# Graph attention over sorted edges: features turned three blocks ahead, and the PSUM banks divided anew

## The chip, the cores and the metric

The kernel runs on one core of a Trainium2 chip. The metric is the device time of one execution in microseconds (us), lower is better. Five engines work side by side, each through its own list of instructions in order: PE (TensorE, matrix products and transposes), DVE (VectorE), ACT (ScalarE), POOL (GpSimd) and SP (SyncE, which here only issues DMAs). They wait for each other through semaphores. SBUF is the large on-chip memory; PSUM is the small one that PE writes into, and it has eight banks, each of which holds 512 float32 values per partition.

## The reference, cut to what matters

There are 12,500 nodes with 128 features and 212,500 edges, sorted by their destination. A node has 8 heads of 16 dimensions.

```python
h = relu(layernorm(x))
q, v = h @ Wq.T + bq, h @ Wv.T + bv            # one row per node
k = edge_attr @ Wk.T + bk                      # one row per edge
qs, qd = q[src], q[dst]
in_m, out_m, diag_m = sum(qs * k), sum(qd * k), sum(qs * qd)      # per head: 24 logits per edge
score = (segment_softmax(in_m / 4, dst) + segment_softmax(out_m / 4, dst)
         + segment_softmax(diag_m / 4, dst)) * distance ** lam
y = segment_sum(score * v[dst], dst)
out = x + leaky_relu(y @ Wo.T + bo, 0.1)
```

The softmax over the edges of one destination needs the largest logit of each destination. Since edges are sorted, these are runs of neighbouring edges.

## The kernel before, in words

The program holds two paths. `ordered_path` always runs; it also looks at the data and writes a flag, and `general_path` runs only if the edges are not as the first path needs them, which they are here.

**Before the loop.** All nodes are loaded and normalized, q is computed for all of them and stored in DRAM in `q_table`. A second table, `q3_table`, holds q as the sum of three bfloat16 terms.

**The tiling of the edges.** 512 edges are one block (`BE`), four edges on each of 128 partitions (`JN` = 4). The 415 blocks of the loop are cut into five strands (`S` = 5) of 83 blocks (`G`). The loop counts steps g; `t = g // 5` is the round and `s = g % 5` the strand. Five blocks, one of each strand, make a round, and what is done once per round handles 5 x 24 = 120 rows: a row of PSUM or SBUF for each strand and logit, along 512 edges.

**What a step does** (lines 1487 to 1547). For the block g + 15 POOL gathers q[src] from `q_table`, 128 rows with each of four indirect DMAs (L691), into one of 22 buffers `qq`. The four are allowed to start after certain PE instructions of earlier steps (`behind`). For the block g + 1 PE computes k into one half of a `kq_ps` tile (`project`, L1155 for the bias and L1157), and q[dst] into the other half (`spread_q`, L1165), the product of a matrix of zeros and ones (`oh`) with the rows of `q3_table` in `win`; ACT copies q[dst] to SBUF as `qd` (L1168). For the block g + 2 PE turns the edge features by four transposes into the PSUM tile `eT_ps` (`turn`, L1148), and ACT copies them to SBUF as `eT` (L1150), from which `project` of the next step takes its weights. For the block g DVE multiplies (`logits`, L1178 and L1179) and, at s = 1, 3 and 4, sums over the 16 dimensions of a head (L1184). ACT makes `oh` for block g + 3 (`one_hots`, L1142 and L1143).

**What a round does.** The logits of a round go through a chain that is spread over the steps of the next two rounds:

- s = 0: PE turns the logits to rows (`turn_logits`, L1205, tile `l_ps`); DVE scans along the edges for the running maximum of each destination (`scan_on`, `u`, L1238), with a row `far` that holds a large negative number where a new destination begins, and a short scan of 64 edges (`head`, L1243). ACT copies `far` to a PSUM tile `far_ps` (`spread_far`, L1249).
- s = 1: DVE scans back, from the last edge to the first (`scan_back`, `m`, L1256), with the row from `far_ps`, where there is one, or else from `far` in SBUF.
- s = 2: PE turns `m` back (`turn_max`, L1326, tile `m_ps`); DVE subtracts (L1334), and ACT takes the exponential (L1335).
- s = 3: PE makes two `d_ps` tiles (`show_ends`, L1360), which ACT turns into zeros and ones (`sel`, L1363 and L1364); DVE multiplies by the edge weights (`weigh_powers`, L1346).
- s = 4: PE sums over the edges of a destination (`to_rows`, L1374, tile `w_ps`), ACT copies the rows (L1379), and SP stores them (L1390).

Between these, nodes whose sums are complete are finished in groups of 512 (`Nodes`, two such groups of steps in most pairs of rounds once enough sums are there): a `node_ps` tile for a transpose at s = 1 (L1074, copied by ACT at L1077) and one for a product at s = 4 (`project_v` and `project_o`, L1080 and L1082). DVE's L1346, L1279, L1282 and L1107 take both operands from SBUF; most of the others take one from PSUM.

**PSUM.** Of the eight banks four belong to the two `kq_ps` tiles, one to `eT_ps`, and three are shared in turn by all small tiles (`small`, L1197): `l_ps`, `far_ps`, `node_ps`, `m_ps`, both `d_ps` and `w_ps`. A new small tile takes the bank of the third before it and waits until that one has been read.

**What sets the order.** `pin` (L596) ties every instruction to the one before it on its engine, so the order on each engine is that of the program text. SP issues the loads in this order too: the edge features of a round are one DMA of 1280 KB (`fetch_edges`, L679, two buffers), the places of the destinations one of 640 KB (`fetch_places`, L636).

**After the loop** (from L1549) the last rounds go through the same chain, and five groups of nodes that could not be finished earlier are (`rest`).

Of the kernel before, what the change touches and what calls it, by code (L numbers as in the profile page):

```python
# [7 lines left out]
F32 = mybir.dt.float32  # L8
# [464 lines left out]
def ordered_path(ctx: ExitStack, tc: tile.TileContext, flag, x, src, dst, edge_attr, edge_weight,  # L473
# [20 lines left out]
    N, F = x.shape  # L494
    E = src.shape[0]
    P = 128
    NI = -(-N // P)
    NP = P * NI
    BE, JN = 512, 4
# [23 lines left out]
    def parts_of(u):  # L523

        return [s for s in range(S)
                if (s == 0 or START * s - NEAR < UN * (u + 1))
                and (s == S - 1 or UN * u <= START * (s + 1) + NEAR)]
# [61 lines left out]
    end = S * G  # L589
# [6 lines left out]
    def pin(inst):  # L596

        engine = str(inst.ins.engine)
        if engine in pinned:
            tc.add_manual_dep(inst.ins, pinned[engine], mybir.DependencyInfo(  # L600
                mybir.DependencyClass.NoSync, mybir.DependencyReason.DATA), reason="in order")
        pinned[engine] = inst.ins.name
        return inst
# [72 lines left out]
    def fetch_edges(t):  # L676
        if t < G:
            ea = eas[t] = load.tile([P, S, JN * F], F32, name="ea")
            pin(nc.sync.dma_start(  # L679
                ea, edge_attr[:end * BE, :].rearrange("(s b p j) f -> p s b (j f)", s=S, b=G, p=P)  # L680
                [:, :, t, :]))

    def gather(g, of=range(JN)):
        if g < end:
            if 0 in of:
                qqs[g] = gath.tile([P, JN, F], F32, name="qq")
            qq = qqs[g]
            s, t = g % S, g // S
            for j in of:
                at = raw_i[:, t, s, j:j + 1] if g < RAW else src_i[:, s * G + t, j:j + 1]  # L690
                rows = pin(nc.gpsimd.indirect_dma_start(  # L691
                    out=qq[:, j, :], out_offset=None, in_=x if g < RAW else q_table,
                    in_offset=bass.IndirectOffsetOnAxis(ap=at, axis=0)))
                if g < RAW:
                    tc.add_manual_dep(rows.ins, pinned[sums_of], mybir.DependencyInfo(
                        mybir.DependencyClass.Sync, mybir.DependencyReason.SCHED_ONLY),
                        reason="one for each group of nodes")
                if (g - LOOK, j) in behind:
                    tc.add_manual_dep(rows.ins, behind[g - LOOK, j], mybir.DependencyInfo(
                        mybir.DependencyClass.Sync, mybir.DependencyReason.SCHED_ONLY),  # L700
                        reason="close behind the products")
# [330 lines left out]
    class Nodes:  # L1032
# [39 lines left out]
        def turn(self, to):  # L1072
            for b in range(self.n):
                pin(nc.tensor.transpose(to[:, b, :], self.h[:, b, :], ident))  # L1074
            if self.hT is None:
                self.hT = fin.tile([P, JN, P], F32, name="hT")
            pin(nc.scalar.copy(self.hT[:, :self.n], to[:, :self.n]))  # L1077
# [48 lines left out]
    with tc.tile_pool(name="work", bufs=2) as work, \  # L1126
            tc.tile_pool(name="scan", bufs=2) as scan, \
            tc.tile_pool(name="ps", bufs=1, space=PSUM) as ps:
        kqs, eTs, qds, ohs, lTs, prods = {}, {}, {}, {}, {}, {}

        def bank(g, i):

            if g not in kqs:
                kqs[g] = ps.tile([P, 2, JN, F], F32, name="kq_ps", bufs=2)
            return kqs[g][:, i]

        def one_hots(g):

            if g < end:
                oh = ohs[g] = work.tile([K3, BE], BF, name="oh", bufs=5)  # L1140
                d = places[g // S][:K3, g % S, :]
                pin(nc.scalar.activation(d, d, AF.Abs, bias=before[:K3]))  # L1142
                pin(nc.scalar.activation(oh, d, AF.Relu, bias=1.0, scale=-1.0))  # L1143

        def turn(g):
            eT_ps = ps.tile([P, JN, P], F32, name="eT_ps", bufs=1)
            for j in range(JN):
                pin(nc.tensor.transpose(eT_ps[:, j, :], eas[g // S][:, g % S, j * F:(j + 1) * F], ident))  # L1148
            eT = work.tile([P, JN, P], F32, name="eT", bufs=2)
            pin(nc.scalar.copy(eT, eT_ps))  # L1150
            eTs[g] = eT

        def project(g):
            k_ps = bank(g, 0)
            pin(nc.tensor.matmul(k_ps, ones3, bk3, start=True, stop=False))  # L1155
            for j in range(JN):
                pin(nc.tensor.matmul(k_ps[:, j, :], eTs[g][:, j, :], wk, start=False,  # L1157
                                     stop=(j == JN - 1)))
            del eTs[g]

        def spread_q(g):
            s, d = g % S, st[g // S]
            qd_ps = bank(g, 1)
            for j in range(JN):
                pin(nc.tensor.matmul(qd_ps[:, j, :], ohs[g][:, j * P:(j + 1) * P],  # L1165
                                     d["win"][:, s, :], start=(j == 0), stop=(j == JN - 1)))
            qds[g] = work.tile([P, JN, F], F32, name="qd")
            pin(nc.scalar.copy(qds[g], qd_ps))  # L1168
            del ohs[g]

# [23 lines left out]
            nc.vector.memset(ends_t[-1][0:1, :], 1.0)  # L1194

        def small(shape, name):
            return ps.tile(shape, F32, name=name, tag="small", bufs=3)  # L1197

        l_end = scan.tile([R, HEAD], F32, name="l_end", bufs=1)
        nc.vector.memset(l_end, 0.0)  # L1200
# [195 lines left out]
        def later(f, t, *more):  # L1396
            if 0 <= t < T:
                f(t, *more)

        def nodes_before(t, s):  # L1400

            new, old = pairs.get(t - t % 2), pairs.get(t - t % 2 - 2)
            if new and t % 2 == 1 and s == 4:
                new.project_v(small([P, JN, F], "node_ps"))
            if old and t % 2 == 0 and s == 4:
                old.project_o(small([P, JN, F], "node_ps"))
# [56 lines left out]

        def hold(of, apart=False):
            if apart:
                of.held = ps.tile([P, JN, F], F32, name="eT_ps", bufs=1)
            else:
                of.held = banks.pop(0)
            of.product(of.held, bv3, wv)
# [12 lines left out]
        project(0)  # L1482
        spread_q(0)
        turn(1)
        one_hots(1)
        one_hots(2)
        for g in range(end):
            s, t = g % S, g // S
            nodes_before(t, s)
            gather(g + LOOK)  # L1490
            if s == 0:
                fetch_edges(t + 1)
            if g + 1 < end:
                project(g + 1)
                behind[g + 1, 0] = pinned[products]
                spread_q(g + 1)
                behind[g + 1, 1] = pinned[products]
            if g + 2 < end:
                turn(g + 2)
                behind[g + 1, 2] = pinned[products]  # L1500
            logits(g)
            one_hots(g + 3)
            if s == 0:
                if t > 0:
                    turn_logits(t - 1)
                    scan_on(t - 1)
                later(select, t - 2)
                later(spread_far, t - 2)
            elif s == 1:
                later(scan_back, t - 2)  # L1510
                if t == 1:
                    logits_few()
            elif s == 2:
                later(turn_max, t - 2)
                later(powers, t - 2)
                fetch_places(t + 2)
            elif s == 3:
                later(show_ends, t - 2)
                later(weigh_powers, t - 2)
                other_terms(t, s)  # L1520
                fetch(t + 2)
            else:
                later(to_rows, t - 2)
            ahead, k = (t + 2, s - 3) if s > 2 else (t + 1, s + 2)
            if ahead > 1:
                fetch_rows(ahead, [k])
            later(put_rows, t - 2 if s == 4 else t - 3, [(s + 1) % S])
            if t == G - 1:
                if 0 < s < 4:
                    select(G - 3 + s)  # L1530
                elif s == 4:
                    for i in (G - 2, G - 1, G):
                        show_ends(i)
            behind[g + 1, 3] = pinned[products]
            nodes_between(t, s)
            if s < 3:
                other_terms(t, s)
            if g == 12 * S:
                examine()
            begin_rest(g - (end - BEGIN))  # L1540
            if g < S:
                of = [u for u in range(NU) if g in parts_of(u)]
                pin(nc.scalar.dma_start(
                    sums[g][of[0] * UN:(of[0] + len(of)) * UN].rearrange(
                        "(n p) i c -> p n (i c)", p=P),
                    blank[:, None, :].to_broadcast([P, 2 * len(of), 2 * 2 * H3])))
# [31 lines left out]
        for r in (2, 3):  # L1578
            hold(rest[r])
# [69 lines left out]
```

## Time and profile before

| | us |
|---|---|
| median of three runs | 2208.59 |
| lowest and highest | 2208.17 and 2213.11 |
| profiled execution | 2207.89 |
| its span, from the first instruction to the last | 2206.0 |
| mean granted TensorE clock | 0.781 of full speed |
| last gather of q[src] starts | 2136.02 |

How to read the profile: a row of the costliest groups has a line of the kernel, the engine, the operation, the tile written and the tiles read, the count, then the busy time of all, the mean of one in ns, and the idle time of the engine just before them with what ended most of it. A row of the waits has the engine, tile and line that waited, what it waited for, and the total, the number and the longest of these waits in us. A row of the timeline has the start, the duration in us, the engine, line, operation and tiles, and in brackets the idle time before it. A row for one line of the kernel has its count and the smallest, median and largest duration in ns, the first and the last start in us, and the shapes. A row of the stretches has the stretch, its length, the busy time and number of the instructions asked for, the granted clock, the DMA share and GB/s.

### The profile page before, as it was taken

How to read it: one execution, taken by the hardware profiler on the slowest of the kernel's cores; microseconds unless marked ns; L12 is line 12 of the kernel's file. 1: busy time of each engine (PE TensorE's matmuls, PEld its weight loads, DVE VectorE, ACT ScalarE, POOL GpSimd, SP SyncE). 2: the span in 40 equal slices, each digit the busy share in tenths (PEclk: the TensorE clock that was granted, in tenths of full speed). 3: DMA queues.
4: the chain of work that ended last, by engine and by line, in shares of the span. 5: the costliest groups of instructions: out<-in, count | busy, mean ns of one | idle time of the engine just before them, and what ended most of it. 6: DMA issues, size and time to landing. Idle time of an engine off the chain costs nothing.

```text
span 2206.0 us, 34366 instructions
## 1 busy us (share of the span) xinstructions
PE 1731.1 (78%) x10289; PEld 1377.7 (62%) x10289; DVE 1953.7 (89%) x2106; ACT 1406.7 (64%) x2617; POOL 1587.6 (72%) x1676
## 2 busy tenths in 40 slices
PE   7678777777887877878887787778887888778886
PEld 5456565665666666656666666666665666666664
DVE  8669999999999998899889999999989898889894
ACT  8656666666666666666666666666666666666671
POOL 3577777777777777777777777777777777777750
PEclk9757888788788788777777778787778777777776
DMA  9585555455455555554555555554556445555531
GB/s 267 165 255 167 159 154 175 143 168 168 145 161 178 159 153 170 163 169 148 155 159 175 164 155 153 178 163 145 162 165 178 149 148 149 172 148 151 154 101 58
DMA packets 306061, 355.65 MB, mean 161 GB/s; under 512 B 118195, under 2 KB 225661, under 8 KB 305557
## 3 DMA queue, kind: packets, MB, share of 16 engines
q1 hardware_dynamic: 237258, 238.26, 35.0%
q0 software_dynamic: 53184, 108.92, 17.4%
q10 hardware_dynamic: 15424, 6.19, 1.1%
q8 instruction: 83, 1.36, 0.3%
q14 instruction: 112, 0.92, 0.1%
HBM read 321.34 MB, written 31.85 MB: 160 GB/s over the span
## 4 chain that ended last, share of the span: by engine, by line
PE 36%; DVE 31%; DMA 13%; issue 11%; ACT 4%; POOL 3%; SPq 1%; DVEq 0%; ACTq 0%; POOLq 0%
PE kq_ps L1157 13%; DMA qq<-q_table,src_i 12%; DVE lT L1184 10%; DVE prod L1179 9%; PE w_ps L1374 6%; PE eT_ps L1148 5%; DVE prod L1178 5%; PE kq_ps L1155 3%; PE node_ps L1082 3%; DVE u L1238 3%; POOL qq L691 3%; PE kq_ps L1165 3%; PE d_ps L1360 2%; ACT xq L919 1%; PE l_ps L1205 1%
## 5 line engine op out<-in xcount | busy, mean ns | idle before, releaser
L691 POOL DMA_INDIRECT qq<-q_table,src_i x1636 | 1557.9, 952 | 505.8 <-issue 242.0
L1157 PEld LDWEIGHTS kq_ps<-wk,eT 128*128 128x128 f32 x3320 | 531.7, 244 | 377.6 <-issue 164.9
L1184 DVE TENSOR_REDUCE lT<-prod 128x192 f32<-128x3072 f32 (+1 forms) x249 | 702.1, 2820 | 8.5
L1157 PE MATMUL kq_ps<-wk,eT 128*128 128x128 f32 x3320 | 628.0, 347 | 11.5 <-ACT eT L1150 10.6
L1168 ACT COPY qd<-kq_ps 128x512 f32<-128x512 f32 x415 | 242.1, 583 | 432.0 <-PE kq_ps L1165 399.2
L1179 DVE TENSOR_TENSOR prod<-qq,kq_ps 128x1024 f32<-128x1024 f32 x415 | 504.1, 1215 | 13.0 <-issue 9.8
L1155 PE MATMUL kq_ps<-b,ones 3*128 3x512 bf16 x415 | 188.0, 453 | 217.3 <-DVE prod L1179 217.1
L1148 PE MATMUL eT_ps<-ident,ea 128*128 128x128 f32 x1660 | 327.3, 333 | 0.6 <-ACT att_t L806 0.6
L1142 ACT ACTIVATE relb<-relb,before 114x512 bf16<-114x512 bf16 x415 | 302.6, 729 | 0.0
L1178 DVE TENSOR_TENSOR prod<-qd,kq_ps 128x512 f32<-128x512 f32 x415 | 280.2, 675 | 12.2 <-ACT qd L1168 7.4
L1143 ACT ACTIVATE oh<-relb 114x512 bf16<-114x512 bf16 x415 | 261.3, 630 | 13.3
L1150 ACT COPY eT<-eT_ps 128x512 f32<-128x512 f32 x415 | 243.8, 588 | 39.4 <-PE eT_ps L1148 38.7
L1148 PEld LDWEIGHTS eT_ps<-ident,ea 128*128 128x128 f32 x1660 | 231.9, 176 | 0.9 <-ACT att_t L806 0.9
L1374 PE MATMUL w_ps<-back,sel 128*114 128x144 f32 (+1 forms) x1344 | 214.4, 321 | 16.0 <-DVE back L1346 10.6
L1374 PEld LDWEIGHTS w_ps<-back,sel 128*114 128x114 f32 (+1 forms) x1344 | 206.7, 212 | 23.3 <-ACT h L1064 5.8
L1326 PE MATMUL m_ps<-ident,m 120*128 120x120 f32 x332 | 70.8, 347 | 169.6 <-DVE m L1256 169.5
L1165 PE MATMUL kq_ps<-win,oh 114*128 114x128 bf16 x1660 | 201.9, 257 | 2.3 <-DMA win<-q_table 2.3
L1238 DVE TENSOR_TENSOR_SCAN u<-far,u,l_ps 120x512 f32<-120x512 bf16 x82 | 104.8, 1278 | 90.9 <-PE l_ps L1205 83.2
L1335 ACT ACTIVATE back<-back 128x480 f32<-128x480 f32 x83 | 50.1, 604 | 200.5 <-DVE back L1334 200.5
L1165 PEld LDWEIGHTS <-oh 114*128 114x128 bf16 x1660 | 162.9, 119 | 15.7 <-issue 2.6
L1326 PEld LDWEIGHTS m_ps<-ident,m 120*128 120x128 f32 x332 | 50.2, 215 | 192.4 <-DVE m L1256 191.2
L1256 DVE TENSOR_TENSOR_SCAN m<-far_ps,head,u 120x512 f32<-120x512 f32 x81 | 103.2, 1274 | 0.0
(192 smaller groups left out, 1435.4 us busy)
## 6 DMA issues: line engine op xcount, KB each, us to landing
ea<-in_edge_attr_dram SPq DMA_DIRECT2D x83, 1280.0 KB
relb<-rel_d SPq DMA_DIRECT2D x83, 640.0 KB
qq<-q_table,src_i POOLq DMA_INDIRECT x1636
win<-q_table SPq DMA_DIRECT2D x415, 28.5 KB
far<-far_d SPq DMA_DIRECT2D x84, 120.2 KB
q_table<-more_q SPq DMA_DIRECT2D x40, 192.0 KB
sums<-rows SPq DMA_DIRECT2D x412, 7.1 KB
q_table<-xq SPq DMA_DIRECT2D x24, 256.0 KB
```

Source lines behind the costliest of these rows:

```text
L691: rows = pin(nc.gpsimd.indirect_dma_start(out=qq[:, j, :], out_offset=None, in_=x if g < RAW else q_table, in_offset=bass.IndirectOffsetOn ...
L1142: pin(nc.scalar.activation(d, d, AF.Abs, bias=before[:K3]))
L1143: pin(nc.scalar.activation(oh, d, AF.Relu, bias=1.0, scale=-1.0))
L1148: pin(nc.tensor.transpose(eT_ps[:, j, :], eas[g // S][:, g % S, j * F:(j + 1) * F], ident))
L1150: pin(nc.scalar.copy(eT, eT_ps))
L1155: pin(nc.tensor.matmul(k_ps, ones3, bk3, start=True, stop=False))
L1157: pin(nc.tensor.matmul(k_ps[:, j, :], eTs[g][:, j, :], wk, start=False, stop=(j == JN - 1)))
L1165: pin(nc.tensor.matmul(qd_ps[:, j, :], ohs[g][:, j * P:(j + 1) * P], d["win"][:, s, :], start=(j == 0), stop=(j == JN - 1)))
L1178: pin(nc.vector.tensor_mul(prod[:, :, 2, :], qds[g], kqs[g][:, 0]))
L1179: pin(nc.vector.tensor_mul(prod[:, :, 0:2, :], qqs[g][:, :, None, :].to_broadcast([P, JN, 2, F]), kqs[g].rearrange("p i j f -> p j i f")))
L1184: pin(nc.vector.tensor_reduce(lTs[t][:, :, lo:s + 1, :].rearrange("p j s c -> p j (s c)"), prods[0][:, :, :s + 1 - lo].rearrange("p j s i ...
L1374: pin(nc.tensor.matmul(w_ps[:, i].rearrange("p s c -> p (s c)"), d["sel"][:n, j, lo:lo + 3, :].rearrange("p s w -> p (s w)"), d["back"][:n ...
```

## The change

It has four parts. `turn` runs for block g + 3 instead of g + 2, with two `eT_ps` banks and four `eT` buffers, and a set of transposes moves ahead of the loop; `qd` gets three buffers instead of two. The edge features are fetched at s = 2 for the round after the next instead of at s = 0 for the next one. The small tiles share two banks instead of three. And `spread_far` isn't called any more, so that `scan_back` always takes `far` from SBUF.

```diff
         def turn(g):
-            eT_ps = ps.tile([P, JN, P], F32, name="eT_ps", bufs=1)
+            eT_ps = ps.tile([P, JN, P], F32, name="eT_ps", bufs=2)
...
-            eT = work.tile([P, JN, P], F32, name="eT", bufs=2)
+            eT = work.tile([P, JN, P], F32, name="eT", bufs=4)
...
-            qds[g] = work.tile([P, JN, F], F32, name="qd")
+            qds[g] = work.tile([P, JN, F], F32, name="qd", bufs=3)
...
         def small(shape, name):
-            return ps.tile(shape, F32, name=name, tag="small", bufs=3)
+            return ps.tile(shape, F32, name=name, tag="small", bufs=2)
...
-                of.held = ps.tile([P, JN, F], F32, name="eT_ps", bufs=1)
+                of.held = ps.tile([P, JN, F], F32, name="eT_ps", bufs=2)
...
         turn(1)
+        turn(2)
...
-            if s == 0:
-                fetch_edges(t + 1)
+            if g == 0:
+                fetch_edges(1)
+            if s == 2:
+                fetch_edges(t + 2)
...
-            if g + 2 < end:
-                turn(g + 2)
+            if g + 3 < end:
+                turn(g + 3)
                 behind[g + 1, 2] = pinned[products]
...
                 later(select, t - 2)
-                later(spread_far, t - 2)
```

## The prediction

> **What bounds the kernel now.** I began with the page's busy times and its costliest groups.
>
> ```profile
> span 2206.0 us, 34366 instructions
> PE 1731.1 (78%) x10289; PEld 1377.7 (62%) x10289; DVE 1953.7 (89%) x2106; ACT 1406.7 (64%) x2617; POOL 1587.6 (72%) x1676
> L691 POOL DMA_INDIRECT qq<-q_table,src_i x1636 | 1557.9, 952 | 505.8 <-issue 242.0
> ```
>
> By these DVE is the bound and POOL has room. The waits of POOL say otherwise: once the gathers from q_table run, none before them is longer than 0.3 us, whatever releaser is named.
>
> ```profile
> POOL qq L691 <- issue: 242.0, 794, 0.3
> POOL qq L691 <- DMA qq<-q_table,src_i: 115.6, 379, 0.3
> POOL qq L691 <- PE kq_ps L1165: 28.6, 94, 0.3
> ```
>
> 0.30 us is thus a fixed gap. Next the gathers alone: their rate in one stretch, their number against the blocks multiplied by DVE (L1179) up to 400 us and from 1300 us on, and the end of the loop in the timeline.
>
> ```profile
> 400.00:1000.00 600.00, 454.42 (x478) 0.79 0.53 162
> ...
> L691 POOL DMA_INDIRECT qq<-q_table,src_i x252: 940/944/2768, 78.2 to 399.5; - x126
> L1179 DVE TENSOR_TENSOR prod<-qq,kq_ps x61: 1202/1214/1218, 111.1 to 396.7; 128x1024 f32<-128x1024 f32 x61
> ...
> L691 POOL DMA_INDIRECT qq<-q_table,src_i x669: 940/944/1367, 1299.3 to 2136.0; - x168
> L1179 DVE TENSOR_TENSOR prod<-qq,kq_ps x169: 1205/1215/1222, 1299.8 to 2134.4; 128x1024 f32<-128x1024 f32 x169
> ...
> 2136.02 0.94 POOL L691 DMA_INDIRECT qq<-q_table,src_i  x1 [0.30 <-issue]
> 2140.07 1.21 DVE L1179 TENSOR_TENSOR prod<-qq,kq_ps 128x1024 f32<-128x1024 f32 x1
> ```
>
> Undisturbed a gather comes every 0.944 + 0.303 = 1.247 us; measured it is 600 / 478 = 1.255, from 78.2 us to 2137. A block takes four, so 5.02 us, and a round of five blocks 25.1 us. At 400 us the gathers of (252 + 24) / 4 = 69 blocks were out (24 are the raw ones before the loop) and 61 blocks multiplied: POOL led by 8. After 1300 us both go at one pace (669 / 4 = 167 against 169), and DVE's last product starts 3 us after the last gather has been issued. **POOL is the bound**, a saturated chain from 78 to 2137 us. DVE is close behind it, and I read its waits to see how close.
>
> ```profile
> DVE u L1238 <- PE l_ps L1205: 83.2, 49, 4.0
> DVE prod L1179 <- issue: 9.8, 5, 2.4
> DVE prod L1179 <- DMA qq<-q_table,src_i: 3.2, 4, 1.2
> PE kq_ps L1157 <- ACT eT L1150: 10.6, 5, 4.1
> ```
>
> Only 9.8 + 3.2 = 13 us of DVE's idle time stand at the product that takes the gathered rows. Without them DVE's own chain would have ended at about 2140 - 13 = 2127 us. Two chains of nearly equal length: whatever lengthens either one shows. The profiled execution took 2207.89 us (span and 1.9 us around it), 0.7 under the median of 2208.59; I add to 2207.9.
>
> **The turning three blocks ahead.** The same 415 x 4 transposes and copies run in the same places of each step; one set moves ahead of the loop. What it can remove is PE's wait for a turned block: 10.6 us, 5 times (above). The much longer waits of the weight loads at the same line overlap the bias product and are not PE's. I take 0; at most -10.6, on DVE's chain only. The two eT buffers, the third qd and the ACT copy of far (0.58 us x 81) are no cost: ACT is busy 64%. Every POOL instruction stays where it was, and no gather waits for the PE steps that release it. The edge load moves two steps later in a round but a round further ahead, past the SP queue's places and node transfers; its first reader comes five blocks after it instead of three. It then goes out just ahead of the 640 KB of relb, so gathers issued then land later, which DVE notices only where it is close behind POOL: 0, at most 5 us.
>
> **No decay row: the scan now reads SBUF twice.** Back over the block, m (L1256) took the row from PSUM; now it takes far itself. The trace has this form twice, after the loop.
>
> ```profile
> L1256 DVE TENSOR_TENSOR_SCAN m<-far_ps,head,u x81: 1273/1274/1275, 175.6 to 2130.3; 120x512 f32<-120x512 f32 x81
> L1256 DVE TENSOR_TENSOR_SCAN m<-far,head,u x2: 1284/1284/1284, 2149.4 to 2151.4; 120x512 f32<-120x512 bf16 x2
> ...
> 1013.00 1.27 DVE L1256 TENSOR_TENSOR_SCAN m<-far_ps,head,u 120x512 f32<-120x512 f32 x1
> 1013.87 0.94 POOL L691 DMA_INDIRECT qq<-q_table,src_i  x1 [0.30 <-issue]
> ```
>
> For DVE that is 10 ns x 81 = 0.8 us. No gather runs beside those two, so the price for POOL has to come from other DVE operations with two operands in SBUF. A gather that starts inside one of them is long; one inside the present m (1013.87) is not:
>
> ```profile
> 92.71 2.29 DVE L844 SCALAR_TENSOR_TENSOR of<-dst_r 104x2048 bf16<-104x2048 int32 x1 [2.03 <-ACT of L841]
> 93.05 2.77 POOL L691 DMA_INDIRECT qq<-q_table,src_i  x1 [0.30 <-issue]
> ...
> 1046.44 0.65 DVE L1346 TENSOR_TENSOR back<-back,att_t 128x480 f32<-128x480 f32 x1
> 1046.53 1.37 POOL L691 DMA_INDIRECT qq<-q_table,src_i  x1 [0.30 <-DVE lT L1184]
> ...
> 1626.54 0.29 DVE L1243 TENSOR_TENSOR_SCAN head<-far,u 120x64 f32<-120x64 bf16 x1
> 1626.60 0.98 POOL L691 DMA_INDIRECT qq<-q_table,src_i  x1 [0.31 <-DMA qq<-q_table,src_i]
> ```
>
> At L844 1.95 us of the operation were left when the gather started, and it took 2.77 - 0.944 = 1.83 longer; at L1346 0.56 left, 0.43 longer; at L1243, the same scan over 64 elements, 0.23 left, 0.04 longer. So the gather is held until 0.12 to 0.19 us before the operation's end. The new m holds for 1.284 - 0.13 = 1.15 us of each 1.247: a hit nearly every time, 1.15 x 1.15 / (2 x 1.247) = 0.53 us on average, 43 us for 81. With 0.19 it is 1.09, 0.48 and 39 us. The same sum for L1346 (0.52 us held) gives 0.108 x 83 = 9 us. All gathers together are 1557.9 - 1636 x 0.944 = 13.5 us long, of which L844 has 1.8, and L1346 is the commonest of several such operations; so the sum is rather too high than too low. **I take 36 us.** Low end: the short scan hardly shows its hold; if a hold grows only by what it showed there (0.06 + 0.04 us for 64 elements, so 0.8 for 512) it is 0.26 x 81 = 21 us. High end: the beats of POOL and DVE lock and each hit is a bad one, 0.75 x 81 = 61. POOL's chain has no slack, so its last gather moves to 2137 + 36 and the last product to about 2176 us.
>
> The Trainium skill (SBUF — State Buffer, "SBUF: two separate sides") has a rule for this: a DVE operation with two SBUF inputs and GpSimd exclude each other at a shared port pair for a whole instruction. The stretched gathers agree. It also says that the one that starts first keeps the pair, so that DVE would wait for a running gather; that is a rival below.
>
> **Two banks for small products.** With three, a product reuses the bank of the third before it; with two, the second before. In a round with node work the order is d_ps, d_ps, node_ps (L1080), w_ps: node_ps, which took the bank of m_ps, now needs that of the first d_ps, which ACT reads (L1363) behind two copies and two activations.
>
> ```profile
> 1712.13 0.81 PE L1360 MATMUL d_ps<-shows,ends_t 21*128 21x380 bf16 x2
> 1712.74 0.63 PE L1080 MATMUL node_ps<-b,ones 3*128 3x512 bf16 x1
> 1714.01 0.84 ACT L1363 ACTIVATE sel<-d_ps 128x380 f32<-128x380 f32 x2
> ...
> 1723.56 0.60 PE L1205 MATMUL l_ps<-ident,lT 128*120 128x128 f32 x4
> 1724.20 1.28 DVE L1238 TENSOR_TENSOR_SCAN u<-far,u,l_ps 120x512 f32<-120x512 bf16 x1 [3.16 <-PE l_ps L1205]
> ...
> L1080 PE MATMUL node_ps<-b,ones x44: 278/629/630, 576.2 to 2196.4; 3*128 3x512 bf16 x43, 3*128 3x256 bf16 x1
> ```
>
> The first of ACT's two reads ends at 1714.01 + 0.48 = 1714.49, so PE stalls 1.75 us at 1712.74. Queued behind are two blocks' projections, w_ps and l_ps, for which u waits; here it would wait 3.16 + 1.75. Of the 44 such products 6 come after the loop: 38 x 1.75 = 66 us at most on DVE's chain. u waits in 49 of 83 rounds; in the others PE has slack, so the low end is 66 x 49 / 83 = 39. DVE's chain then ends at 2127 + 39 = 2166 to 2127 + 66 = 2193. Other reuses (d_ps after m_ps, l_ps after node_ps) find readers that finished earlier in the same order: 0, up to 5.
>
> **The tail.** After the last gather 2206 - 2137 = 69 us follow, with chains of small products: six d_ps in turn with ACT, l_ps behind them, m_ps three times, five project_o whose bank is free only after DVE's maximum. Each costs about one ACT or DVE step of 0.5 to 0.7 us, and few are on the path: 4 us, bounds 0 and 7.
>
> **The sum.** The loop ends with the later chain: POOL's at 2176, DVE's between 2166 and 2193. Halfway from 2176 to 2193 is 2184, 44 us after 2140. 2207.9 + 44 + 4 = 2256 us.
>
> **The rivals.**
> - The scan holds nothing, since it is a scan: POOL ends at 2137, and DVE's chain alone sets the end, 2166 to 2193, middle 2180: 2207.9 + 40 + 4 = 2252. For it speaks only how little L1243 shows; against it, that it shows something.
> - The two prices add instead of covering each other (a held gather delays DVE, PE's stall then comes on top): up to 36 + 66 + 4, from 2270 to 2314. This needs DVE to wait for gathers most rounds, while today that is 13 us.
> - DVE waits for gathers too: 0.944 of 1.247 us are covered, 0.36 us on average, x 81 = 29 us, on DVE's chain 2180 + 29 = 2209, so 2281. This is the rule's other half. Against it: L1346 and the short scan at L1243 are never longer than 717 and 349 ns, medians 649 and 291.
>
> ```profile
> L1346 DVE TENSOR_TENSOR back<-back,att_t x84: 645/649/717, 184.2 to 2159.4; 128x480 f32<-128x480 f32 x83, 16x480 f32<-16x480 f32 x1
> L1243 DVE TENSOR_TENSOR_SCAN head<-far,u x83: 291/291/349, 170.3 to 2151.1; 120x64 f32<-120x64 bf16 x83
> ```
>
> - Not slower: the beats lock the good way. Where DVE waits for gathers, its products start a fixed time after a gather lands, and m follows the reduction at a fixed distance, so at one phase of POOL's beat. If this phase lets the next gather start in the 0.10 to 0.15 us of the beat that m leaves free, each hit costs under 0.05 us, 4 in all; and DVE, which then follows POOL, takes PE's stall out of time in which it would wait for rows. The time is 2208 to 2212. It decides only if DVE is tied to the gathers from early on, and today it leads to 13 us of waiting, all late. Far below 2208 nothing can go: 1636 x 1.247 = 2040 of POOL's 2059 us remain.
>
> **How the numbers follow.** Forecast 0.62, holding nothing 0.11, adding up 0.12, both held 0.05, not slower 0.08, something faster 0.02. A difference under 0.3% (6.6 us) can't be told from none: faster 0.02, same 0.06, slower 0.92. Range: from 21 us of hold and little stall, 2230, to the lower part of the adding case, 2286.
>
> **What would show it.** Gathers that start inside m are up to 1.1 us long and POOL's busy time rises by some 36 us, its other gaps staying 0.30; a wait of PE at L1080's product for ACT's L1363 near 1.75 us appears about 38 times; u's wait for l_ps grows from 83 us; L1256 reads 1284 ns; the eT waits vanish without a trace in the time. Wrong would be: gathers of unchanged length inside m, or a last gather at 2137 us.

## The result, and the profile after

The changed kernel took 2271.18 us in the median of four runs (2269.81 to 2281.53), the kernel before 2209.36 beside it. The ratio is 1.0285, with a 95% interval of 1.0273 to 1.0298: slower by 62 us, within the range and 15 us above the forecast of 2256. The profiled execution took 2272.32 us.

The page of the changed kernel, its span, busy times and the group of the gathers:

```profile
span 2270.5 us, 34425 instructions
PE 1712.4 (75%) x10289; PEld 1366.8 (60%) x10289; DVE 1956.4 (86%) x2106; ACT 1372.7 (60%) x2536; POOL 1620.2 (71%) x1676
L691 POOL DMA_INDIRECT qq<-q_table,src_i x1636 | 1590.4, 972 | 505.7 <-issue 247.2
```

POOL has 32.5 us more to do for the same 1636 gathers (1590.4 against 1557.9), its idle time before them is the same. ACT has lost its 81 copies. Next the rows by line (count, smallest, median and largest duration in ns, first and last start in us), with where the two chains end:

```profile
L691 POOL DMA_INDIRECT qq<-q_table,src_i x1636: 940/944/2762, 78.2 to 2168.4; - x182
L1179 DVE TENSOR_TENSOR prod<-qq,kq_ps x415: 1201/1212/1217, 111.5 to 2202.5; 128x1024 f32<-128x1024 f32 x139
L1256 DVE TENSOR_TENSOR_SCAN m<-far,head,u x83: 1273/1274/1284, 180.8 to 2214.8; 120x512 f32<-120x512 bf16 x83
```

The last gather starts 32.4 us later than before (2168.4 against 2136.0), DVE's last product 62.4 us later (2202.5 against 2140.1). The two ends now lie 34 us apart instead of 4: POOL sets the end of the loop no longer. What follows the last product takes 2270.5 - 2202.5 = 68.0 us against 65.9. The waits show what holds DVE up:

```profile
DVE u L1238 <- PE l_ps L1205: 133.1, 59, 4.3
PE node_ps L1080 <- ACT sel L1363: 61.3, 38, 1.9
DVE prod L1178 <- ACT qd L1168: 32.2, 22, 3.6
POOL qq L1460 <- DVE prod L1179: 18.9, 4, 6.5
PE kq_ps L1157 <- ACT eT L1150: 4.2, 1, 4.2
```

The row of the kernel before for qd:

```profile
DVE prod L1178 <- ACT qd L1168: 7.4, 6, 3.9
```

PE's wait for the bank of the first d_ps is new: 38 times, 61.3 us. DVE waits 50 us more for l_ps (133.1 against 83.2) and 25 us more for qd (32.2 against 7.4), and nowhere for gathered rows, where it waited 13 us before. These three changes add up to 61.7 us, and DVE's last product moved by 62.4. POOL waits for DVE after its last gather. Both prices can be seen in the timeline, a gather that starts inside the scan, and a product that stands until ACT has read the first of two tiles:

```profile
1014.41 1.27 DVE L1256 TENSOR_TENSOR_SCAN m<-far,head,u 120x512 f32<-120x512 bf16 x1
1015.10 1.34 POOL L691 DMA_INDIRECT qq<-q_table,src_i  x1 [0.30 <-issue]
...
1761.84 0.81 PE L1360 MATMUL d_ps<-shows,ends_t 21*128 21x380 bf16 x2
1763.72 0.84 ACT L1363 ACTIVATE sel<-d_ps 128x380 f32<-128x380 f32 x2
1764.24 0.58 PE L1080 MATMUL node_ps<-b,ones 3*128 3x512 bf16 x1 [1.59 <-ACT sel L1363]
```

When the gather started, 1014.41 + 1.27 - 1015.10 = 0.58 us of the scan were left, and it took 1.34 - 0.944 = 0.40 us longer: held until 0.18 us before the scan's end. Over the whole trace 80 gathers start inside this scan and 65 of them are long, 34.3 us together; each of the 65 is held until 0.19 us (0.188 to 0.197) before the scan's end.

### The profile page after: what moved, and what is told of

Read it like the earlier page. It is cut to its first block, busy times and chain, and to the rows that moved or that the text cites. A ratio compares the mean times of both kernels' runs of the same rounds, so it can differ in the third digit from the quotient of the medians.

```text
span 2270.5 us, 34425 instructions
## 1 busy us (share of the span) xinstructions
PE 1712.4 (75%) x10289; PEld 1366.8 (60%) x10289; DVE 1956.4 (86%) x2106; ACT 1372.7 (60%) x2536; POOL 1620.2 (71%) x1676
## 4 chain that ended last, share of the span: by engine, by line
PE 39%; DVE 30%; ACT 12%; DMA 8%; issue 7%; POOL 2%; DVEq 0%; SPq 0%; ACTq 0%; POOLq 0%
PE kq_ps L1157 14%; DVE lT L1184 11%; DVE prod L1179 9%; DMA qq<-q_table,src_i 8%; PE w_ps L1374 7%; PE eT_ps L1148 5%; DVE prod L1178 5%; PE kq_ps L1155 4%; PE node_ps L1082 3%; PE kq_ps L1165 3%; ACT relb L1142 2%; ACT oh L1143 2%; POOL qq L691 2%; ACT eT L1150 2%; DVE u L1238 2%
## 5 line engine op out<-in xcount | busy, mean ns | idle before, releaser
L691 POOL DMA_INDIRECT qq<-q_table,src_i x1636 | 1590.4, 972 | 505.7 <-issue 247.2
L1184 DVE TENSOR_REDUCE lT<-prod 128x192 f32<-128x3072 f32 (+1 forms) x249 | 702.1, 2819 | 8.6
L1178 DVE TENSOR_TENSOR prod<-qd,kq_ps 128x512 f32<-128x512 f32 x415 | 279.6, 674 | 37.3 <-ACT qd L1168 32.2
L1155 PEld LDWEIGHTS <-ones 3*128 3x128 bf16 x415 | 39.8, 96 | 300.0 <-DVE prod L1179 262.1
L1238 DVE TENSOR_TENSOR_SCAN u<-far,u,l_ps 120x512 f32<-120x512 bf16 x82 | 104.8, 1278 | 133.6 <-PE l_ps L1205 133.1
```

Source lines behind the costliest of these rows:

```text
L691: rows = pin(nc.gpsimd.indirect_dma_start(out=qq[:, j, :], out_offset=None, in_=x if g < RAW else q_table, in_offset=bass.IndirectOffsetOn ...
L1178: pin(nc.vector.tensor_mul(prod[:, :, 2, :], qds[g], kqs[g][:, 0]))
L1184: pin(nc.vector.tensor_reduce(lTs[t][:, :, lo:s + 1, :].rearrange("p j s c -> p j (s c)"), prods[0][:, :, :s + 1 - lo].rearrange("p j s i ...
```

## The experiments

The question was which of the two prices, the hold of POOL and the stall of PE, makes the 62 us, whether they add or cover each other, and whether turning ahead does anything.

**The hold alone.** The changed kernel with three small banks and one eT_ps bank:

```diff
-            eT_ps = ps.tile([P, JN, P], F32, name="eT_ps", bufs=2)
+            eT_ps = ps.tile([P, JN, P], F32, name="eT_ps", bufs=1)
...
-            return ps.tile(shape, F32, name=name, tag="small", bufs=2)
+            return ps.tile(shape, F32, name=name, tag="small", bufs=3)
...
```

> Small tiles have three banks again, eT_ps one; still no decay row, still turned three blocks ahead. The hold of POOL alone. Theory (the loop ends with the later of two chains, POOL's with the holds and DVE's with PE's stall): no wait at L1080, gathers 32 us longer in all as in the changed kernel (1590 us busy), last gather near 2169, last L1179 3 us after it, time 2236 to 2248. Rival 1 (only the stall matters, the hold is covered): 2207 to 2214. Rival 2 (turning ahead or the moved edge load costs by itself): above 2252.

Measured: 2237.8 us, ratio 1.0114 (1.0083 to 1.0145). Its rows, from the page, by line and from the waits:

```profile
L691 POOL DMA_INDIRECT qq<-q_table,src_i x1636 | 1585.7, 969 | 505.8 <-issue 245.4
...
L691 POOL DMA_INDIRECT qq<-q_table,src_i x1636: 940/944/2754, 78.2 to 2163.8; - x182
L1179 DVE TENSOR_TENSOR prod<-qq,kq_ps x415: 1200/1214/1224, 111.6 to 2168.7; 128x1024 f32<-128x1024 f32 x139
...
DVE prod L1179 <- DMA qq<-q_table,src_i: 37.8, 29, 3.6
```

With the stall gone POOL is the bound again: DVE waits 37.8 us for rows, and the last product starts 5 us after the last gather. The hold is 1585.7 - 1557.9 = 27.8 us, and the last gather 27.8 us later. Both rivals fall.

**The stall alone.** Two small banks as in the changed kernel, one eT_ps bank, and the free bank for far_ps:

```diff
...
-            far_ps = st[t]["far_ps"] = small([R, BE], "far_ps")
+            far_ps = st[t]["far_ps"] = ps.tile([R, BE], F32, name="far_ps", bufs=1)
...
                 later(select, t - 2)
+                later(spread_far, t - 2)
```

> The decay row is back, in a bank of its own; small tiles keep two banks, eT_ps has one. The stall of PE alone. Theory (later of two chains): wait at L1080 38 times, some 61 us; gathers as before the change (1558 us busy), last gather near 2137; last L1179 near 2200, time 2264 to 2274, so as the changed kernel, because there the hold is covered. Rival (the two prices add): 2271 less the 32 us of hold, 2234 to 2244.

Measured: 2274.32 us, ratio 1.0277 (1.0251 to 1.0303), as the changed kernel and 0.3 us above the expected span. From the page, by line and from the waits:

```profile
L691 POOL DMA_INDIRECT qq<-q_table,src_i x1636 | 1559.7, 953 | 508.2 <-issue 249.3
...
L691 POOL DMA_INDIRECT qq<-q_table,src_i x1636: 940/944/2767, 79.8 to 2140.1; - x182
L1179 DVE TENSOR_TENSOR prod<-qq,kq_ps x415: 1201/1214/1217, 113.2 to 2204.1; 128x1024 f32<-128x1024 f32 x139
...
PE node_ps L1080 <- ACT sel L1363: 61.0, 38, 1.9
POOL qq L1460 <- DVE prod L1179: 48.9, 4, 32.0
```

Without the hold the gathers are as short as before and end at 2140, but DVE's last product starts at 2204 as it did with the hold. So the stall alone makes the changed kernel's time, and the hold is covered by it.

**The stall taken out of the changed kernel.** Only the product of the node groups at s = 4 moves, to the second eT_ps bank:

```diff
-                new.project_v(small([P, JN, F], "node_ps"))
+                new.project_v(ps.tile([P, JN, F], F32, name="eT_ps", bufs=2))
...
-                old.project_o(small([P, JN, F], "node_ps"))
+                old.project_o(ps.tile([P, JN, F], F32, name="eT_ps", bufs=2))
```

> The changed kernel with one thing different: the product of the node groups at s = 4 (L1080) is put into the second eT_ps bank instead of one of the two small ones. Theory: the wait of L1080 for L1363 is gone (under 5 us), DVE's u waits some 50 us less, POOL's chain with the holds sets the end: last gather near 2169, time 2238 to 2250. Rival (other reuses of the two banks cost as much): 2258 or more, the waits having moved to L1205, L1360 or L1374.

Measured: 2247.5 us, ratio 1.0157 (1.0137 to 1.0177). From the page, by line and from the waits:

```profile
L691 POOL DMA_INDIRECT qq<-q_table,src_i x1636 | 1596.9, 976 | 505.9 <-issue 252.3
...
L691 POOL DMA_INDIRECT qq<-q_table,src_i x1636: 940/944/2856, 78.8 to 2175.4; - x182
...
DVE u L1238 <- PE l_ps L1205: 54.2, 34, 4.3
DVE prod L1179 <- DMA qq<-q_table,src_i: 61.2, 42, 2.8
```

The wait at L1080 is gone, and with it 24 us, though the other small tiles still share two banks. POOL is the bound, and its last gather starts at 2175.4. It is 10 us slower than the kernel with three banks, and the gathers say why: they are 11 us longer (1596.9 against 1585.7). The expected 2169 us for the last gather was missed by 6 us. The gathers of the three kernels with the hold are 28, 32.5 and 39 us longer than before. The gathers that start inside the scan make 31.8, 34.3 and 39.7 us of stretch there, so the difference lies with the 81 scans themselves; that it is the place where they fall in POOL's beat is the likely reason, but was not tried.

**The turning alone.** Three small banks, one eT_ps bank and the row in PSUM as before; what stays of the change is the turning, the buffers and the edge load:

```diff
...
-            return ps.tile(shape, F32, name=name, tag="small", bufs=2)
+            return ps.tile(shape, F32, name=name, tag="small", bufs=3)
...
                 later(select, t - 2)
+                later(spread_far, t - 2)
```

> Turned three blocks ahead, edge load moved, four eT and three qd buffers; three small banks, decay row as before, one eT_ps bank. Theory: POOL's chain sets the end, last gather 2136 to 2138, time 2205 to 2212, no difference from before. Rival (turning ahead or the moved edge load costs by itself): 2218 or more. Rival (it shortens PE's chain and that shows): below 2202.

Measured: 2212.72 us, ratio 1.0006 (0.9995 to 1.0017): no difference, though 0.7 us above the expected span. In its profile, though, DVE waited 39.6 + 2.2 us for gathered rows instead of 13, as if its own chain had become shorter behind POOL's. So both kernels were profiled once more, unchanged.

> The kernel before, unchanged, for a second profile: how much the waits of DVE vary by themselves. If turning ahead shortened DVE's chain, this one waits for gathers some 13 us as in the first profile, and u some 83 us for l_ps; if the granted clock of the run made the difference, anything up to 40 us can stand there with a clock over 0.79.

> turn_ahead_alone, unchanged, for a second profile. If turning ahead shortened DVE's chain, DVE waits for gathers some 40 us again, whatever the granted clock; if the clock of 0.806 did, near 13 us at a clock near 0.785.

The waits of DVE, first in the second profile of the kernel before (2212.39 us, clock 0.788), then in the first and the second of the turning alone (2213.34 us at 0.806, 2217.03 at 0.781):

```profile
DVE u L1238 <- PE l_ps L1205: 73.8, 45, 4.3
DVE prod L1179 <- issue: 12.6, 6, 3.8
DVE prod L1179 <- DMA qq<-q_table,src_i: 8.9, 7, 2.4
```

```profile
DVE u L1238 <- PE l_ps L1205: 60.8, 41, 4.1
DVE prod L1179 <- DMA qq<-q_table,src_i: 39.6, 28, 3.2
DVE prod L1179 <- issue: 2.2, 3, 0.9
```

```profile
DVE u L1238 <- PE l_ps L1205: 104.5, 53, 4.2
```

The second profile of the turning alone has no wait for rows at all, and its u waits 104.5 us. So the 40 us do not repeat, and the kernel before varies too (13 and 21.5 us). In both kernels the execution with the lower granted clock has the longer wait of u; with two executions of each, that the clock is the cause is not shown. A gain from turning ahead was not seen; a small one on DVE's chain would not be seen under this variation. The two chains are so close that they change places: in this second profile the last gather starts at 2139.4 us and DVE's last product at 2149.2, so there DVE's chain ended the loop.

**Shorter holds.** If the price of a hold goes with the square of the operation's duration, as the sum in the prediction has it, cutting the operations that read SBUF twice makes POOL faster. L1346, L1107, L1279 and L1282 were cut in halves, L839 and L844 in quarters, first on the turning alone, then on the kernel before:

```diff
...
-            pin(nc.vector.tensor_mul(back[:n, :, :, 1, :], back[:n, :, :, 0, :],
-                                     att[:n].to_broadcast([n, JN, S, H3])))
+            for j in range(0, JN, 2):
+                pin(nc.vector.tensor_mul(back[:n, j:j + 2, :, 1, :], back[:n, j:j + 2, :, 0, :],
+                                         att[:n, j:j + 2].to_broadcast([n, 2, S, H3])))
...
```

> turn_ahead_alone with DVE operations that read SBUF twice cut into shorter ones: L1346, L1107, L1279 and L1282 in halves, L839 and L844 in quarters. Theory (a gather that starts inside such an operation waits for its end, so the price goes with the square of the duration): the gathers, 1558.6 us busy there, lose two thirds of their 14 us of stretch and come to 1547 to 1551; last gather near 2130; DVE's chain, some 20 us longer through the additional instructions, stays hidden behind POOL's, since turning ahead left it 42 us of waiting for gathers: time 2201 to 2207 against 2212.7, ratio to before 0.995 to 0.998. Rival (the price goes with the number of operations): 1558 or more, 2211 to 2218.

> The kernel before with the same operations cut, so without turning ahead. Theory: gathers 1547 to 1551 us busy, last gather near 2128, but DVE's chain has only 13 us of waiting for gathers to give for its 20 us of additional work: last L1179 10 us or more after the last gather, time 2205 to 2215, ratio 0.998 to 1.003. Rival (DVE's slack is no limit): as fast as turn_ahead_split.

Measured: 2204.42 us with turning ahead, ratio 0.9973 (0.9963 to 0.9984), and 2204.77 us without, ratio 0.9969 (0.9957 to 0.9981), beside 2210.32 of the kernel before. Both beat both uncut kernels, by 0.3%. The profiled execution with turning ahead was the slowest of its nine, 2213.93 us. The gathers on the page and by line and DVE's product (now L1184), first with turning ahead, then without:

```profile
L691 POOL DMA_INDIRECT qq<-q_table,src_i x1636 | 1553.6, 950 | 506.1 <-issue 273.7
...
L691 POOL DMA_INDIRECT qq<-q_table,src_i x1636: 940/944/1679, 78.7 to 2132.0; - x182
L1184 DVE TENSOR_TENSOR prod<-qq,kq_ps x415: 1202/1214/1218, 113.3 to 2148.2; 128x1024 f32<-128x1024 f32 x139
...
L1355 DVE TENSOR_TENSOR back<-back,att_t x168: 391/400/460, 190.2 to 2167.2; 128x240 f32<-128x240 f32 x166, 16x240 f32<-16x240 f32 x2
```

```profile
L691 POOL DMA_INDIRECT qq<-q_table,src_i x1636 | 1552.5, 949 | 505.7 <-issue 270.4
...
L691 POOL DMA_INDIRECT qq<-q_table,src_i x1636: 940/944/1959, 78.1 to 2130.5; - x182
L1184 DVE TENSOR_TENSOR prod<-qq,kq_ps x415: 1201/1214/1218, 113.4 to 2139.8; 128x1024 f32<-128x1024 f32 x139
```

The direction was right, the size not: over 1636 x 0.944 = 1544.4 us the stretch went from 13.5 or 14.2 us to 8.1 or 9.2, by 35 to 40%, not by two thirds. In the second profiles of the uncut kernels the gathers were 17 us over it (1561.3 and 1561.4), so the fall is known only to lie between a third and a half. One reason is in the rows: a half of L1346 (now L1355) takes 400 ns and not 325.

The gain in time is not the gathers' alone. In both profiles DVE has no wait for rows, and its last product starts 16 and 9 us after the last gather: DVE's chain ends the loop now. What follows that product takes 63.9 and 63.3 us, against 65.9 to 66.1 in the four profiles of the uncut kernels, so some 2 to 3 of the 5.5 to 5.9 us lie behind the loop. The second kernel did come out without slack on DVE, as expected, but was as fast as the first and 0.2 us below its expected span, which fits the finding that turning ahead gives DVE's chain nothing.

**Half of the stall.** The changed kernel with project_v alone in the second eT_ps bank. It came to a chip on which the kernel before took 2669.69 us instead of 2210, with a granted clock of 0.73 to 0.75, and was run again there beside the changed kernel.

> The changed kernel with project_v alone put into the second eT_ps bank; project_o keeps a small bank. Half of the stalls at L1080 are gone: 18 to 20 waits, 29 to 32 us. Theory (the loop ends with the later of two chains): DVE's chain shrinks from 2202 by some 30 us to about 2172, POOL's ends near 2170 as before; last L1179 between 2172 and 2185, time 2242 to 2254. Rival (the loop follows the stalls alone, each costing its 1.6 us): 2271 - 31 = 2240 here, and the kernel without any stall would be at 2210, which node_product_in_eT_bank was not. Rival (the first half costs nothing or the second nothing): near 2271 or near 2247.

> half_the_stall, unchanged, beside the changed kernel on one chip. On a chip that grants PE the clock of the first profiles (near 0.79, the kernel before near 2210): 18 to 20 waits at L1080, last L1179 between 2172 and 2185, time 2242 to 2254 if the loop ends with the later of two chains; 2240 with no further gain from the other half if it follows the stalls alone. On a chip like that of half_the_stall (clock near 0.73, before near 2670) PE's products set the pace, gathers wait for PE, and half_the_stall and changed kernel differ by the stalls alone, some 30 us.

> The changed kernel, unchanged, on the same chip as half_the_stall_again. Near 0.79 of the clock: 2268 to 2276, ratio 1.026 to 1.031. Near 0.73: PE sets the pace, holds of POOL are covered, the ratio is that of 62 us of stall to 2670, 1.02 to 1.03.

Measured: half of the stall 2708.73 us, ratio 1.0154 (1.0132 to 1.0176); again 2681.5 us, 1.0134 (1.0109 to 1.0160), with 2645.55 for the kernel before; the changed kernel 2712.58 us, 1.0274 (1.0234 to 1.0314). The changed kernel on this chip, from the page, by line and from the waits:

```profile
PE 1852.8 (69%) x10289; PEld 1456.5 (54%) x10289; DVE 1963.5 (73%) x2106; ACT 1364.0 (51%) x2536; POOL 1608.5 (60%) x1676
L691 POOL DMA_INDIRECT qq<-q_table,src_i x1636 | 1578.6, 965 | 900.2 <-issue 366.3
...
L691 POOL DMA_INDIRECT qq<-q_table,src_i x1636: 939/946/2769, 78.1 to 2551.0; - x182
L1179 DVE TENSOR_TENSOR prod<-qq,kq_ps x415: 1201/1214/1217, 111.3 to 2625.9; 128x1024 f32<-128x1024 f32 x139
...
POOL qq L691 <- remote: 146.6, 103, 5.3
PE node_ps L1080 <- ACT sel L1363: 71.6, 18, 8.3
```

Here POOL stands idle for 900 us before its gathers instead of 506, and the last product comes 75 us after the last gather: POOL is not the bound, and the hold is covered. What sets the pace on this chip is not shown. The granted clock of this execution is lower than in the first profile of this kernel (0.722 against 0.790), but PE is busy only 140 us longer in a span that is 423 us longer, and many waits, 146.6 us of POOL's among them, have no releaser on this core in the profile (`remote`). Half of the stall costs 36 to 39 us and all of it 67, so here the price is about proportional. The waits behind it are not those expected: L1080 waits for L1363 9 and 7 times in the two profiles of half the stall (43.5 and 29.6 us), not 18 to 20 times, and 18 times in the changed kernel, not 38. What half the stall makes where POOL is close behind, which is what the run was meant for, stays open.

## Why the prediction was right, and where it was off

- **POOL's chain is the bound before, and has no slack: right.** With the hold alone the gathers took 27.8 us more, the last one came 27.8 us later, and the time rose by 27 us, 1.1%. DVE's 89% busy time was not the bound. The margin is thin: one of the two profiles of the turning alone has DVE's chain as the later one.
- **The hold, forecast at 36 us: 32.5 in the changed kernel**, 28 to 39 in the three kernels that have it; the last gather at 2168 against 2173 forecast. The bounds of 21 and 61 held, though the 0.75 us a scan behind the upper one was not worked out; the scans' mean was 0.39 to 0.49 us. The model held too: each gather that is held waits until 0.19 us before the scan's end.
- **The stall, forecast at 1.75 us x 38 = 66 at most: 61.3 us in 38 waits, 1.61 each.** The size was right. The step that was off is how the stall reaches DVE: the low end, "u waits in 49 of 83 rounds; in the others PE has slack", and with it the middle between 2176 and 2193. DVE's chain ended at 2202, above the 2193 that I had as its latest. Two things show in the rows: a stall that does not reach u has another door, the product at s = 0 that waits for qd (32.2 us against 7.4), and the start of the sum, 2127, was that of one execution, in a chain that varies by tens of us between executions (the waits of u were 83 and 74 us in two profiles of the kernel before, 61 and 105 in two of the turning alone).
- **The loop ends with the later chain, the prices cover each other: right.** Stall alone 1.0277, both 1.0285, hold alone 1.0114. The rival in which they add falls, and the one without a hold as well. The time by itself could not have told: 2271 us also lies in the 2270 to 2314 of the rival in which they add, and only the run with the stall alone separates the two.
- **DVE waits for a running gather: wrong, as expected.** In the loop the new scan keeps its 1274 ns; the 1284 ns that were forecast for it are those of the two scans behind the loop, so the 0.8 us of DVE did not come either. This is the point where the rule of the Trainium skill (SBUF — State Buffer, "SBUF: two separate sides") and the rows part: POOL is held for nearly the whole operation of DVE, but DVE loses little to a gather. No recurring DVE operation with both operands in SBUF is more than 0.08 us above its median: in the changed kernel L1346 takes up to 716 ns against 653, L1024 up to 408 against 333.
- **Not slower, through a lucky phase: wrong.** In the changed kernel 65 gathers are held in the scan, 34 us together, and DVE is not tied to the gathers.
- **Turning ahead, the buffers and the edge load at nothing: right**, 1.0006 (0.9995 to 1.0017). PE's waits for eT went from 10.6 to 4.2 us.
- **The tail, forecast at 4 us: 2.1** (68.0 against 65.9).

## What to carry to other kernels

An engine with 72% busy time can be the bound: look at whether any of its waits is longer than its fixed gap before looking at shares. Where POOL issues indirect DMAs without a pause, a DVE operation with both operands in SBUF takes time from it that grows faster than the operation's duration: here 0.39 to 0.49 us for a scan of 1.27 us, 0.06 to 0.11 us for an L1346 of 0.65 us in the kernels without the hold. The square in the sum is a model that fits this roughly. One operand in PSUM gave the time back; cutting operations in halves and quarters gave back a third to a half of it. When a shared ring of banks loses one, go through the order of its tiles and ask for each whose reader now stands between: one new pair (here node_ps behind d_ps) can cost more than all that the freed bank brings.

## What the runs showed of the hardware

The hold has a sharp edge that I had not expected to be so even: in the changed kernel a gather that starts while 0.58 us of the scan are left is 0.40 us longer, one beside the same scan with its row in PSUM not at all (1013.87 in the profile before, and none of the 82 that start inside that scan there). The small loss of DVE has its place too: of the 84 runs of L1346 in the changed kernel 39 take more than 665 ns, and each of these starts within 0.03 us of the start of a gather. And the time of one kernel can differ by a fifth between chips: the kernel before took 2210 us at granted clocks of 0.78 to 0.80 on some and 2646 to 2670 us at 0.73 to 0.75 on another, and the ratio of the changed kernel was nearly the same, 1.0285 and 1.0274. POOL was not the bound of the changed kernel in either profile; the kernel before was not profiled on the slower chip, and what makes that chip slower is open.
